# Layer 0's Gram matrices from float16 halves, a planner that knows of eight loads in flight, and a first batch turned row by row

## The chip, the cores and the metric

The kernel runs on one core of one Trainium2 chip. The metric is the device time in microseconds of one execution; the median of three runs is compared. PE is TensorE, DVE VectorE, ACT ScalarE, POOL GpSimd, SP SyncE. POOL issues the DMAs that convert a type, and SP most others.

## The reference, cut to what matters

Four graph layers work on `x` (16 batches of 1024 nodes with 128 features) and `adj` (16 x 1024 x 1024, zeros and ones). The change lies in layer 0:

```python
h = jnp.maximum(_layernorm(x, axis=-1), 0.0)
adjT = jnp.transpose(adj.astype(jnp.float32), (0, 2, 1))
w = _masked_row_softmax(adjT)                         # equal shares over a node's neighbours
region = jnp.matmul(w, h)
region = jnp.matmul(region, kernel_1) + bias_1        # 128 -> 256
region = _batch_norm(region, gamma_1, beta_1)         # mean and variance over all 16 x 1024 nodes
people = jnp.matmul(jnp.transpose(w, (0, 2, 1)), region)
people = jnp.matmul(people, kernel_2) + bias_2        # 256 -> 128
people = _batch_norm(people, gamma_2, beta_2)
x = x + people
```

Layers 1 to 3 are attention layers on the same `adj`.

## The kernel before

Since `adj` holds only zeros and ones, the softmax is a division by a node's number of neighbours. The kernel never forms `region @ kernel_1`. Both batch norms are worked out from sums: a 128x128 matrix of sums of squares and products (a Gram matrix) and column sums of the aggregated features, one pair for each norm. From these `norms` makes one folded 128x128 matrix, and only then can layers 1 to 3 start.

`first_layer` calls `batch(b)` sixteen times. A batch works as follows, with its steps by name and line:

- `load` (L372, POOL) brings eight blocks `a` of 128 rows of `adj`, 512 KB of int32 each, into 128 KB of 8-bit floats. There are 18 places for `a`. `load_x` (L366) brings the batch of x.
- `stats`, `aggregate` (L382, L386, DVE), `power` (L389, L390, POOL), `centre` (L394, DVE): layer norm. `upper` (L398, POOL) applies the ReLU and rounds to float16, `lower` (L401, DVE) keeps what the rounding left. The two float16 halves and a column of ones form `hv`, 257 wide.
- `turn` (L418, PE) transposes the blocks, 32 times 128x128. In each of four banks all eight blocks must be there. `square` (L426, ACT) writes the transposed matrix `at` and sums its rows, 8 times 1024 columns.
- `share` (L434 to L437, DVE) makes the reciprocals `rc`.
- `product` (L459, PE): eight blocks of eight matrix products with `hv`. Behind each block: `low` (L463, ACT), `join` (L467, DVE), giving `r`; then `high` (L471, POOL) and `rest` (L474, DVE) split `r` into the float16 halves `rv`.
- `spread` (PE, through `gram_product`, L352): eight float32 products of `r` with itself and a column of ones, added up in the bank `gram[0]` over all batches.
- `product2` (L499, PE): eight blocks of eight products of `at` with `rv`, 259 wide; `low2` (L503, ACT), `join2` (L506, DVE) give `g`; `spread2` adds up `gram[1]` (L352); `turn2` and `save` (L533 PE, L536 ACT) turn `g` back, and SP stores it.

Six banks `ps` hold the results of PE; the other two are the Gram matrices.

The order is not written by hand. `Plan` collects the steps, each with an engine, a duration in microseconds as the planner assumes it, and what it reads and writes. `attempt` lists the steps per engine: of those that could start within `L0_WITHIN` of the earliest, it takes the one with the smallest rank, which is the batch's due time (`L0_DUES`) less the length of the chain behind it. It also places the buffers. Instructions are then emitted in this order, and each engine runs its own in order. `norms` puts its steps in the same plan. `plain_layers` (layers 1 to 3) makes a plan of its own.

Before the plan, POOL writes the identity, the columns of ones and the constants (L242 to L344), and the loads follow.

Of the kernel before, what the change touches and what calls it, by code (L numbers as in the profile page):

```python
# [9 lines left out]
F16 = mybir.dt.float16  # L10
# [21 lines left out]

UP = 2.0**12
LEVEL = 1638.0
XG_TILES = 6
WEIGHTS_AT = 40.0
WHOLE = 4
L0_DUES, L0_WITHIN = [
    3.2, 51.2, 72.4, 90.5, 112.6, 124.5, 191.4, 204.9, 159.2, 265.6, 223.0, 273.4, 306.2, 325.8, 419.8, 408.3,
    419.5, 419.5,  # L40
], 0.1
# [173 lines left out]
def gnn_stack(ctx: ExitStack, tc: tile.TileContext, x, adj, k1, b1, g1, be1, k2, b2, g2, be2,  # L215
# [11 lines left out]
    ident = const.tile([P, P], F32, name="ident")  # L227
    make_identity(nc, ident)
    ident_h = const.tile([P, P], F16, name="ident_h")
    nc.vector.tensor_copy(ident_h, ident)  # L230
    ones = const.tile([P, P], F32, name="ones")
# [9 lines left out]
    rows9 = const.tile([P, P], BF16, name="rows9")  # L241
    nc.gpsimd.memset(rows9, 0.0)  # L242
    qall = const.tile([P, B, NB], F32, name="qall")
    q9_all = const.tile([P, B * NB * 9 + P - 9], BF16, name="q9_all")
    q9 = q9_all[:, : B * NB * 9].rearrange("p (b k c) -> p b k c", b=B, c=9)
    nc.gpsimd.memset(q9_all, 1.0)

# [60 lines left out]
def first_layer(tc, rooms, x, adj, adj_t, gt_rows, qall, ident, ident_h, mhalf, held):  # L308
# [7 lines left out]
    def places(kind, count, shape, dtype):  # L316
# [11 lines left out]
        "g": places("g", 2, [P, NB, D + 2], F32),  # L328
        "t": places("t", 2, [P, NB, D + 2], F32),
        "st": places("sta", 3, [P, NB, 6], F32),  # L330
        "mv": places("mva", 3, [P, NB, 2], F32),
# [5 lines left out]
    for t in kinds["hv"]:  # L337
        nc.gpsimd.memset(t[:, :, 2 * D : 2 * D + 1], 1.0)
    for t in kinds["rv"]:
        nc.gpsimd.memset(t[:, :, W2 - 1 : W2], 1.0)  # L340
    for t in kinds["r"]:
        nc.gpsimd.memset(t[:, :, D : D + 1], 1.0)
    for t in kinds["g"]:
        nc.gpsimd.memset(t[:, :, D + 1 : D + 2], 1.0)  # L344
    level = pool.tile([P, 1], F32, name="level")
    nc.vector.memset(level, -LEVEL)
    plan = Plan(kinds)
    plan.gram, plan.okay = gram, okay
    fresh = [True, True]

    def gram_product(k, lhs, rhs):
        nc.tensor.matmul(gram[k][:, : rhs.shape[1]], lhs, rhs, start=fresh[k], stop=True, skip_group_check=True)  # L352
        fresh[k] = False

    def batch(b):
# [9 lines left out]
        def load_x():  # L365
            queue.dma_start(xb.ap.rearrange("p (w t) d -> p w t d", t=2), x[b].rearrange(PAIRED, p=P, t=2))  # L366

        if b == 0:
            step(engine, us_, load_x, (), [xb, ("xo", b)], P * N * 4)
        for j in range(NB):  # L370
            def load(j=j):
                nc.gpsimd.dma_start(rows[j].ap, adj[b].rearrange(PAIRS_OF_ROWS, p=P, t=2)[j // 2, j % 2])  # L372

            step("pool", 0.6, load, (), [rows[j]], P * N * 4)
            if b and j == 1:
                step(engine, us_, load_x, [("xo", b - 1)], [xb, ("xo", b)], P * N * 4)

# [19 lines left out]
        def upper():  # L397
            nc.gpsimd.tensor_scalar_max(hv.ap[:, :, 0:D], y.ap, 0.0)  # L398

        def lower():  # L400
            nc.vector.scalar_tensor_tensor(hv.ap[:, :, D : 2 * D], y.ap, 0.0, hv.ap[:, :, 0:D],  # L401
                                           ALU.max, ALU.subtract)
# [4 lines left out]
        step("dve", 2.3, centre, [xb, mv, rs], [y])  # L407
        step("pool", 2.9, upper, [y], [(hv, 0)])
        step("dve", 1.2, lower, [y, (hv, 0)], [(hv, 1)])

        at, sums, rc = room("at"), room("col"), room("col")
        for w in range(NB // 2):
            ps = room("ps")

            def turn(w=w, ps=ps):
                t = ps.ap.bitcast(F16)
                for j in range(NB):
                    nc.tensor.transpose(t[:, j * P : (j + 1) * P],  # L418
                                        rows[j].ap.bitcast(F16)[:, w * P : (w + 1) * P], ident_h)

            step("pe", 0.47, turn, rows, [ps])
            for t in range(2):
                i = 2 * w + t

                def square(i=i, t=t, ps=ps):
                    nc.scalar.activation(at.ap[:, i, :], ps.ap.bitcast(F8)[:, t::2], AF.Square,  # L426
                                         saturate=False, accum_out=sums.ap[:, i : i + 1])

                step("act", 1.22, square, [ps], [(at, i), (sums, i)])

# [22 lines left out]
        for i in range(NB):  # L453
# [24 lines left out]
            def spread(i=i):  # L478
                gram_product(0, r.ap[:, i, :D], r.ap[:, i, :])

            step("pe", 0.95, product, [*rows, (hv, 0), (hv, 1)], [ps])
            step("act", 0.36, low, [ps, rc], [(t1, i)])
            step("dve", 0.29, join, [ps, rc, (t1, i)], [(r, i)])
            step("pool", 0.6, high, [(r, i), rc], [(rv, i, 0)])
            step("dve", 0.33, rest, [(r, i), rc, (rv, i, 0)], [(rv, i, 1)])
            step("pe", 0.23, spread, [(r, i)], [("gram", 0, b, i)])

# [6 lines left out]
        for j in range(NB):  # L494
            ps = room("ps")

            def product2(j=j, ps=ps):
                for i in range(NB):
                    nc.tensor.matmul(ps.ap[:, :W2], at.ap[:, i, j * P : (j + 1) * P],  # L499
                                     rv.ap[:, i, :], start=(i == 0), stop=(i == NB - 1))  # L500

            def low2(j=j, ps=ps):
                nc.scalar.copy(t2.ap[:, j, :], ps.ap[:, D + 1 : W2])  # L503

            def join2(j=j, ps=ps):
                nc.vector.tensor_tensor(g.ap[:, j, : D + 1], ps.ap[:, : D + 1], t2.ap[:, j, : D + 1],  # L506
                                        ALU.add)

            def spread2(j=j):
                gram_product(1, g.ap[:, j, :D], g.ap[:, j, :])  # L510

            step("pe", 0.95, product2,
                 [*((at, i) for i in range(NB)), *((rv, i, k) for i in range(NB) for k in (0, 1)), (rv, "c")],
                 [ps])
            step("act", 0.21, low2, [ps], [(t2, j)])
            step("dve", 0.25, join2, [ps, (t2, j)], [(g, j)])
            step("pe", 0.23, spread2, [(g, j)], [("gram", 1, b, j)])

        def open_rows():
            nc.vector.tensor_single_scalar(okay[:, b, 1, :], t2.ap[:, :, D + 1], 0.5, op=ALU.is_ge)  # L520

# [6 lines left out]
        for js in groups_of(NB, 4):  # L528
            ps = room("ps")

            def turn2(js=js, ps=ps):
                for k, j in enumerate(js):
                    nc.tensor.transpose(ps.ap[:, k * P : (k + 1) * P], g.ap[:, j, :D], ident)  # L533

            def save(js=js, ps=ps):
                nc.scalar.copy(gtr.ap[:, js[0] * P : (js[-1] + 1) * P], ps.ap)  # L536

            step("pe", 0.46, turn2, [(g, j) for j in js], [ps])
            step("act", 0.56, save, [ps], [(gtr, js[0])])
# [14 lines left out]
def norms(nc, plan, w, qall, q9, rows9, ident, ones, mhalf, gat1, gat3, edge, shift, kcs, flag, count):  # L554
# [100 lines left out]
    s1, v1, mean1, raw1, var1, sq1 = (tile_of(n, CB) for n in ("s1", "v1", "mean1", "raw1", "var1", "sq1"))  # L655
    dve(lambda: V.tensor_scalar_mul(cov, gram[0][:, : P + 1], UP**-2 / count), all1, [cov], 0.3)
    t3, m1 = plan.room("ps"), plan.room("ps")
# [10 lines left out]
    m2 = plan.room("ps")  # L668
    pe(means, [cov], [m1], 0.6)
    dve(lambda: V.tensor_tensor(gk, t3.ap[:, : CB * P], w["k1"], ALU.mult), [t3], [gk], 0.4)  # L670
# [23 lines left out]
    u9 = tile_of("u9", P)  # L694
    dve(lambda: V.tensor_scalar(u9[:9], u[:9], masks[:9, 3:4], 1.0 / UP, ALU.mult, ALU.mult), [u, "masks"], ["u9"], 0.2)
    dve(lambda: V.tensor_copy(uc, tc_.ap[:, 0:1]), [tc_], [uc])
# [5 lines left out]
    def q_sums():  # L702
        V.tensor_tensor(q2, qf, qf, ALU.mult)
        V.tensor_reduce(qs[:, 0:1], qf, AX.X, ALU.add)
        V.tensor_reduce(qs[:, 1:2], q2, AX.X, ALU.add)
        V.tensor_scalar_mul(qs[:, 0:1], qs[:, 0:1], 1.0 / UP / count)
        V.tensor_scalar_mul(qs[:, 1:2], qs[:, 1:2], UP**-2 / count)

# [21 lines left out]
    cov2, gk2, gq, gsum = tile_of("cov2", P), tile_of("gk2", P), tile_of("gq"), tile_of("gsum")  # L730
    dve(lambda: V.tensor_scalar_mul(cov2, gram[1][:, :P], UP**-2 / count), all2, [cov2], 0.25)
    dve(lambda: V.tensor_scalar_mul(gq, gram[1][:, P : P + 1], 2.0 * UP**-2 / count), all2, [gq])
    dve(lambda: V.tensor_scalar_mul(gsum, gram[1][:, P + 1 : P + 2], 1.0 / UP / count), all2, [gsum])
    t5, m3, m4 = plan.room("ps"), plan.room("ps"), plan.room("ps")
# [22 lines left out]
    pe(lambda: T.matmul(t7.ap[:, :P], ones, diag[1], start=True, stop=True), [diag[1]], [t7])  # L757
    dve(lambda: V.scalar_tensor_tensor(kcs, kc, 1.0 / UP, t6.ap[:, :P], ALU.mult, ALU.mult), [t6, kc], [kcs], 0.25)
    whole, rest2 = tile_of("whole", P), tile_of("rest2", P)
# [917 lines left out]
```

## Time and profile before

| what | value |
|---|---|
| median of three runs | 1424.29 us (1423.61 to 1425.9) |
| the profiled execution, its own time | 1423.44 us |
| span of its trace | 1421.6 us |
| granted TensorE clock, mean | 0.998 of full speed |
| PE, weight loads, DVE, ACT, POOL busy, share of the span | 97, 89, 77, 56, 25% |
| first transposition, first `product` | 7.44 us, 23.71 us |
| last Gram product of layer 0 | starts 362.27 us, takes 1.96 us |
| `product`, 64 matrix products of a batch | 7.18 us |
| `product2`, 64 | 7.24 us |
| one Gram matrix, one batch, 8 float32 products | 1.79 us |

The timeline lists groups of equal instructions with their start, their length from the first start to the last end, and in brackets the idle time in front of them with what ended it. The chain of waits follows the last instruction back to the first, and gives the starts and lengths of its pieces. A float32 matrix product shows as two instructions. A line that ends in "ld" for PE is a weight load, which overlaps the product before it.

### The profile page before, as it was taken

To read this page: it belongs to the slowest core of one execution; us is meant where nothing else is said; L and a number is where in the kernel's file an instruction comes from. 1 tells how busy PE (TensorE), PEld (TensorE's weight loads), DVE (VectorE), ACT (ScalarE), POOL (GpSimd) and SP (SyncE) were. 2 spreads that over 40 slices of the span, in tenths; PEclk is the share of its full clock that TensorE was granted. 3 is DMA by queue.
4 is the path that set the end of the run, shared out by engine and by line. 5 is a ranking of instruction groups with operands and counts; after the bars stand their busy time and mean duration, and the time that the engine had idled before them with its cause. 6 is when DMAs were issued, how large, how long until landed. Compare 5 with 4: busy or idle time off the path is not lost.

```text
span 1421.6 us, 30420 instructions
## 1 busy us (share of the span) xinstructions
PE 1373.0 (97%) x11710; PEld 1262.9 (89%) x11710; DVE 1100.7 (77%) x3148; ACT 794.2 (56%) x2123; POOL 358.9 (25%) x469
## 2 busy tenths in 40 slices
PE   4999999999999999999999999999999999999997
PEld 3889899899898898998899898998989998998897
DVE  4877666454688889887889788887888798977786
ACT  3766766666545645636374645546374655346643
POOL 7877676562210110201011101101011111020000
PEclk9999999999999999999999999999999999999999
DMA  9999887870300002121111112021221110000011
GB/s 157 146 186 170 116 167 149 112 99 7 119 2 16 31 31 75 46 90 60 46 60 46 64 41 75 31 80 47 84 60 60 60 46 31 31 1 16 16 44 65
DMA packets 56379, 99.05 MB, mean 70 GB/s; under 512 B 6328, under 2 KB 45600, under 8 KB 52896
## 3 DMA queue, kind: packets, MB, share of 16 engines
q1 hardware_dynamic: 37504, 79.17, 15.8%
q0 software_dynamic: 18720, 17.83, 14.5%
q8 instruction: 94, 1.54, 0.4%
q14 instruction: 61, 0.50, 0.1%
HBM read 118.37 MB, written 28.95 MB: 104 GB/s over the span
## 4 chain that ended last, share of the span: by engine, by line
PE 82%; DVE 8%; ACT 4%; POOL 2%; DMA 2%; issue 1%; DVEq 0%; ACTq 0%; POOLq 0%
PE psc L957 43%; PE psc L1100 7%; PE psa L499 7%; PE psa L459 7%; PE gram L352 4%; PE psc L1004 3%; PE psc L1132 3%; PE psc L933 2%; PE psa L418 2%; PE psc L882 1%; DVE xg L1068 1%; DMA a<-in_adj_dram 1%; DVE eu L1118 1%; ACT y L929 1%; POOL hv L398 1%
## 5 line engine op out<-in xcount | busy, mean ns | idle before, releaser
L957 PE MATMUL psc<-v,xg 128*128 128x129 f32 x4096 | 482.6, 275 | 1.3 <-DVE xg L1068 1.2
L957 PEld LDWEIGHTS psc<-v,xg 128*128 128x128 f32 x4096 | 471.7, 192 | 13.1 <-issue 7.3
L957 PEld LDWEIGHTS psc<-h,xg 128*128 128x128 f32 x2048 | 239.1, 192 | 16.9 <-DVE xg L1136 8.9
L957 PE MATMUL psc<-h,xg 128*128 128x129 f32 x2048 | 247.9, 276 | 3.8 <-DVE xg L1136 3.3
L915 POOL TENSOR_SCALAR col<-mv 128x8 f32<-128x8 f32 x48 | 20.9, 434 | 868.1 <-DVE mv L910 800.8
L1068 DVE SCALAR_TENSOR_TENSOR xg<-ub,tri,at 128x1024 f32<-128x1024 f32 x176 | 217.5, 1276 | 4.3 <-DMA at<-adj_t 2.9
L1108 ACT ACTIVATE eu<-psc,edge_shift 128x512 f32<-128x512 f32 x192 | 113.6, 592 | 173.5 <-PE psc L1100 173.0
L426 ACT ACTIVATE at<-psa 128x1024 fp8e4<-128x1024 fp8e4 x128 | 131.2, 1033 | 45.1 <-PE psa L418 43.3
L1100 PE MATMUL psc<-gt,gt 128*128 128x512 f32 (+3 forms) x384 | 150.9, 492 | 5.3 <-DVE xg L1136 4.0
L1118 DVE SCALAR_TENSOR_TENSOR eu<-e,edge_shift,eu 128x1024 f32<-128x1024 f32 (+7 forms) x128 | 104.0, 812 | 38.0 <-ACT e L1104 36.8
L459 PE MATMUL psa<-hv,a 128*128 128x257 f16 x1024 | 120.7, 277 | 3.3 <-DVE hv L401 3.3
L499 PE MATMUL psa<-rv,at 128*128 128x259 f16 x1024 | 120.0, 275 | 2.7 <-DVE g L506 2.2
L459 PEld LDWEIGHTS <-a 128*128 128x128 fp8e4 x1024 | 101.4, 99 | 19.1 <-issue 3.5
L499 PEld LDWEIGHTS <-at 128*128 128x128 fp8e4 x1024 | 99.6, 98 | 19.1 <-issue 3.6
L929 ACT ACTIVATE y<-xg,col 128x128 f32<-128x128 f32 x256 | 79.1, 400 | 65.1 <-DVE col L912 65.1
L1104 ACT ACTIVATE e<-psc,edge_shift 128x512 f32<-128x512 f32 x192 | 113.6, 592 | 0.0
L1068 DVE SCALAR_TENSOR_TENSOR xg<-ub,tri,atc 128x1024 f32<-128x1024 f32 x80 | 99.2, 1275 | 6.0 <-DMA ub<-u_rows 3.8
L1156 ACT ACTIVATE y<-psc,col 128x128 f32<-128x128 f32 x256 | 69.2, 419 | 56.5 <-DVE col L1150 56.3
L471 POOL TENSOR_SCALAR rv<-r,cola 128x128 f16<-128x128 f32 x128 | 82.0, 650 | 61.2 <-DVE r L467 61.0
L981 ACT ACTIVATE y<-psc,col 128x128 f32<-128x128 f32 x256 | 71.9, 394 | 45.3 <-DVE col L975 39.2
L916 POOL TENSOR_TENSOR col<-col,mhalf 128x8 f32<-128x8 f32 x48 | 94.1, 1961 | 4.0
L1060 ACT ACTIVATE v<-psc,col 128x128 f32<-128x128 f32 x256 | 72.4, 394 | 26.6 <-DVE col L1020 22.8
(209 smaller groups left out, 1941.9 us busy)
## 6 DMA issues: line engine op xcount, KB each, us to landing
a<-in_adj_dram POOLq DMA_DIRECT2D x128, 128.0 KB, 7.2
ub<-u_rows SPq DMA_DIRECT2D x29, 512.0 KB, 4.0
xb<-in_x_dram SPq DMA_DIRECT2D x27, 512.0 KB, 6.8
adj_t<-at SPq DMA_DIRECT2D x13, 1024.0 KB, 4.9
at<-adj_t SPq DMA_DIRECT2D x8, 1024.0 KB
out_dram<-y SPq DMA_DIRECT2D x15, 512.0 KB, 3.9
gt_rows<-xg SPq DMA_DIRECT2D x13, 512.0 KB, 5.6
xg<-gt_rows SPq DMA_DIRECT2D x13, 512.0 KB, 3.9
```

The costliest lines, as they stand in the source:

```text
L426: nc.scalar.activation(at.ap[:, i, :], ps.ap.bitcast(F8)[:, t::2], AF.Square, saturate=False, accum_out=sums.ap[:, i : i + 1])
L459: nc.tensor.matmul(ps.ap[:, : 2 * D + 1], block[:, i % 2 :: 2], hv.ap[:, j, :], start=(j == 0), stop=(j == NB - 1))
L471: nc.gpsimd.tensor_scalar_mul(rv.ap[:, i, 0:D], r.ap[:, i, :D], rc.ap[:, i : i + 1])
L499: nc.tensor.matmul(ps.ap[:, :W2], at.ap[:, i, j * P : (j + 1) * P], rv.ap[:, i, :], start=(i == 0), stop=(i == NB - 1))
L916: nc.gpsimd.tensor_tensor(rs.ap, va.ap, mhalf, ALU.pow)
L929: nc.scalar.activation(y.ap[:, n, :], xs(n), AF.Relu, bias=nm.ap[:, n : n + 1])
L957: nc.tensor.matmul(acc[g].ap[:, k * V1 : (k + 1) * V1], weights[m].ap[:, n * P : (n + 1) * P], values.ap[:, m, :], start=(m == 0 and k == ...
L1068: nc.vector.scalar_tensor_tensor(q[m].ap, ub.ap, ex.ap[:, m, 1:2], at.ap[:, m, :], ALU.max, ALU.mult)
L1100: nc.tensor.matmul(ps.ap[:, : len(c)], ha.ap[:, m * P : (m + 1) * P], ht.ap[:, m * P + c[0] : m * P + c[-1] + 1], start=True, stop=True)
L1104: nc.scalar.activation(e.ap[:, c[0] : c[-1] + 1], ps.ap[:, : len(c)], AF.Exp, bias=shift[:, 0:1], scale=1.0 - SLOPE)
L1108: nc.scalar.activation(eu.ap[:, ROW[m] + c[0] : ROW[m] + c[-1] + 1], ps.ap[:, : len(c)], AF.Exp, bias=shift[:, 1:2], scale=SLOPE)
L1118: nc.vector.scalar_tensor_tensor(t, e.ap[:, :wide], shift[:, 2:3], t, ALU.max, ALU.mult)
```

## The change

- Gram matrices: for batches 0 to 14 the float32 products go. `halves` splits all of `r` (later `g`) into two float16 halves `hl`: a copy on ACT, a subtraction on DVE, and for `g` two small operations for the column `q`. `gram_halves` makes two float16 products for each of the eight blocks: the first half with both halves and the columns of ones (259 wide), and the second half with itself and these columns (131 wide). All four kinds of products are thus kept. The last batch keeps float32 products (`gram_whole`), as one of 128 columns and one of the one or two others.
- `norms` adds the parts together (`sums`): the parts from batches 0 to 14 are prepared before the last batch's products are in.
- `g` is scaled down by 2^10 in `low2` and `join2` (which becomes a `scalar_tensor_tensor`), and the factors behind it follow (`UPG`).
- The planner: a load depends on the load eight places before it (`IN_FLIGHT`), the assumed durations of several steps and all due times are new.
- The first batch: each block is turned into all four banks as it arrives, and the ReLU is on ACT (`first_upper`) instead of POOL.
- POOL's constants go to DVE, and the identity is made behind the first loads.

```diff
+DOWN = 2.0**-10
+UPG = UP * DOWN
+IN_FLIGHT = 8
 L0_DUES, L0_WITHIN = [
-    3.2, 51.2, 72.4, 90.5, 112.6, 124.5, 191.4, 204.9, 159.2, 265.6, 223.0, 273.4, 306.2, 325.8, 419.8, 408.3,
-    419.5, 419.5,
+    0.3, 13.9, 23.7, 30.7, 41.0, 50.1, 58.8, 68.1, 75.2, 86.2, 96.1, 104.3, 114.0, 122.4, 148.4, 153.3, 151.6,
+    151.6,
 ], 0.1
...
-    make_identity(nc, ident)
-    nc.vector.tensor_copy(ident_h, ident)
-    nc.gpsimd.memset(rows9, 0.0)
+    nc.vector.memset(rows9, 0.0)
-    nc.gpsimd.memset(q9_all, 1.0)
+    nc.vector.memset(q9_all, 1.0)
...
+        "hl": places("hl", 2, [P, NB, 2 * D + 3], F16),
...
-    def gram_product(k, lhs, rhs):
-        nc.tensor.matmul(gram[k][:, : rhs.shape[1]], lhs, rhs, start=fresh[k], stop=True, skip_group_check=True)
+    def gram_add(k, at, lhs, rhs):
+        nc.tensor.matmul(gram[k][:, at : at + rhs.shape[1]], lhs, rhs, start=fresh[k], stop=True, skip_group_check=True)
         fresh[k] = False
+    def gram_whole(k, t, n):
+        gram_add(k, 0, t[:, n, :D], t[:, n, :D])
+        gram_add(k, 2 * D + 2 - k, t[:, n, :D], t[:, n, D:])
+    def gram_halves(k, t, n):
+        c = slice(0, 2 * D + 3)
+        gram_add(k, 0, t[:, n, :D], t[:, n, c])
+        gram_add(k, 2 * D + 3, t[:, n, D : 2 * D], t[:, n, D : 2 * D + 3])
...
+        def begun():
+            sent[0] += 1
+            return ([("sent", sent[0] - IN_FLIGHT)] if sent[0] >= IN_FLIGHT else []), ("sent", sent[0])
...
-            step("pool", 0.6, load, (), [rows[j]], P * N * 4)
+            limit, mine = begun()
+            step("pool", 0.55, load, limit, [rows[j], mine], P * N * 4)
+            if b == 0 and j == 3:
+                step("pool", 0.6, lambda: make_identity(nc, ident), (), ["ident"])
+                step("dve", 0.3, lambda: nc.vector.tensor_copy(ident_h, ident), ["ident"], ["ident_h"])
...
+        def first_upper():
+            nc.scalar.activation(hv.ap[:, :, 0:D], y.ap, AF.Relu)
...
-            step("pe", 0.47, turn, rows, [ps])
+        if b == 0:
+            for j in range(NB):
+                step("pe", 0.25, lambda j=j: turn(range(NB // 2), [j]), [rows[j], "ident_h"], turned)
...
-                step("act", 1.22, square, [ps], [(at, i), (sums, i)])
+                step("act", 1.0, square, [ps], [(at, i), (sums, i)])
...
-            step("pe", 0.23, spread, [(r, i)], [("gram", 0, b, i)])
+            if b == B - 1:
+                step("pe", 0.34, spread, [(r, i)], [("gram", 0, b, i)])
+        def halves(k, t, width):
+            hl = room("hl")
+            def first():
+                nc.scalar.copy(hl.ap[:, :, :D], t.ap[:, :, :D])
+            def second():
+                nc.vector.tensor_tensor(hl.ap[:, :, D : 2 * D], t.ap[:, :, :D], hl.ap[:, :, :D], ALU.subtract)
+                if k:
+                    nc.vector.tensor_copy(hl.ap[:, :, 2 * D + 1], t.ap[:, :, D])
+                    nc.vector.tensor_tensor(hl.ap[:, :, 2 * D], t.ap[:, :, D], hl.ap[:, :, 2 * D + 1], ALU.subtract)
+            step("act", 1.0, first, [(t, i) for i in range(NB)], [(hl, 0)])
+            step("dve", 1.6 if k else 1.2, second, [*((t, i) for i in range(NB)), (hl, 0)], [(hl, 1)])
+            for i in range(NB):
+                step("pe", 0.17, lambda i=i: gram_halves(k, hl.ap, i), [(hl, 0), (hl, 1)], [("gram", k, b, i)])
+        if b < B - 1:
+            halves(0, r, D)
...
-                nc.scalar.copy(t2.ap[:, j, :], ps.ap[:, D + 1 : W2])
+                nc.scalar.mul(t2.ap[:, j, :], ps.ap[:, D + 1 : W2], DOWN)
...
-                nc.vector.tensor_tensor(g.ap[:, j, : D + 1], ps.ap[:, : D + 1], t2.ap[:, j, : D + 1],
-                                        ALU.add)
+                nc.vector.scalar_tensor_tensor(g.ap[:, j, : D + 1], ps.ap[:, : D + 1], DOWN, t2.ap[:, j, : D + 1],
+                                               ALU.mult, ALU.add)
...
-    dve(lambda: V.tensor_scalar_mul(cov, gram[0][:, : P + 1], UP**-2 / count), all1, [cov], 0.3)
+    def sums(k, cov, scale, all_):
+        low = tile_of(f"low{k}", P + 3)
+        early = [a for a in all_ if a[2] < B - 1]
+        act(lambda: S.mul(low, gram[k][:, 2 * P + 3 : 3 * P + 6], scale), early, [low], 0.4)
+        dve(lambda: V.scalar_tensor_tensor(low[:, :P], gram[k][:, P : 2 * P], 2.0 * scale, low[:, :P], ALU.mult, ALU.add),
+            [low, *early], [low], 0.35)
+        dve(lambda: V.scalar_tensor_tensor(cov[:, :P], gram[k][:, :P], scale, low[:, :P], ALU.mult, ALU.add),
+            [low, *all_], [cov], 0.35)
+        return low
```

## The prediction

> **What bounds it now.** I read the page first, then the window table of layer 0 in steps of 20 us, the chain of waits, the timeline of the first 60 us, and single groups. Times: the profiled execution took 1423.44 us, its span is 1421.6, and the median of the runs is 1424.29, 0.85 above the profiled one; I sum against the profiled run and add 0.85 at the end.
>
> The page's busy line and its chain, by engine, come first.
>
> ```profile
> PE 1373.0 (97%) x11710; PEld 1262.9 (89%) x11710; DVE 1100.7 (77%) x3148; ACT 794.2 (56%) x2123; POOL 358.9 (25%) x469
> ...
> PE 82%; DVE 8%; ACT 4%; POOL 2%; DMA 2%; issue 1%; DVEq 0%; ACTq 0%; POOLq 0%
> ```
>
> TensorE sets the time. The window table shows where that holds in layer 0.
>
> ```profile
> 0.00:20.00 20.00, 4.45 (x31) 3.17 (x32) 4.64 (x29) 3.40 (x6) 14.07 (x36) 1.00 0.95 115
> 20.00:40.00 20.00, 16.70 (x142) 13.87 (x141) 14.61 (x54) 13.31 (x30) 16.02 (x18) 1.00 0.96 182
> 40.00:60.00 20.00, 17.91 (x163) 15.71 (x162) 17.82 (x89) 11.08 (x28) 16.03 (x22) 1.00 1.05 188
> ...
> 160.00:180.00 20.00, 20.00 (x196) 18.08 (x194) 12.56 (x55) 14.18 (x33) 13.64 (x20) 1.00 1.00 166
> 180.00:200.00 20.00, 20.00 (x196) 18.20 (x194) 12.79 (x55) 14.14 (x34) 13.95 (x20) 1.00 0.92 163
> ```
>
> The columns are PE, weight loads, DVE, ACT, POOL, granted clock, DMA share. From about 51 us to 351 PE is full and the clock whole: a us taken off PE there is a us gained, as long as nothing else becomes late. Before 51 us PE has holes, so the head is ruled by latency. The chain gives PE's prices per batch.
>
> ```profile
> 59.11 1.79 PE psa L418 x32
> ...
> 188.14 7.24 PE psa L499 x64
> 195.38 1.79 PE gram L352 x16
> 198.04 7.18 PE psa L459 x64
> ```
>
> A batch is 1.79 (turning) + 7.18 + 7.24 + 2 x 1.79 (both Gram matrices) + 1.04 (L533, eight in 1.04 in the timeline) = 20.8 us.
>
> **Gram products of batches 0 to 14.** Eight float32 products take 1.79, 0.224 each, in two instructions each. The new pair is a float16 product 259 wide and one 131 wide. L499 is exactly 259 wide with a float16 moving side: 7.24/64 = 0.113. L418 is the nearest to 131: 1.79/32 = 0.056 for 128, so 0.057. Eight pairs: 8 x 0.170 = 1.36, a saving of 0.43 per matrix and batch, 30 times: **-12.8 us**, all in the full stretch. Both rows include their weight loads. I keep 0.40 to 0.45 as bounds, 12.0 to 13.5.
>
> **What pays for it.** Each matrix adds an ACT copy of 128x1024 (L1084, 1.06) and a DVE subtraction (L401, same size, 1.23), g's also two 128x8 operations (L435, 0.20). `join2` becomes the form of `join`: 0.35 for 0.29, 0.5 in eight. Per batch DVE gets 2.5 + 0.4 + 0.5 = 3.4 on 13.5 (51.52 busy in 160 to 240 us, per 20.8), ACT 2.1 on 14.8, in a new period of 20.0: 84% each. PE covers it, so the work costs nothing unless it is late.
>
> Late for whom? In the changed order PE does, behind the last block of `product`, g's pairs of the batch before (1.36), its turning back (1.04) and 24 turns (1.34): 3.7 us, then r's pairs. These need the last `low` (0.46), `join` (0.35), the copy (1.06) and the subtraction (1.23), and three hops of 0.1 (a `join` ended at 179.16, its `high` began at 179.26): 3.4; in some batches DVE's queue has `full` and the statistics (1.64) in front of the subtraction, which started behind `join` makes 4.3. So 0 to 0.6 a batch is exposed, and `product2` waits in line behind r's pairs. Float32 products needed only `join`. I take 0.17 a batch, **+2.6 us**, bounds 0 and 9.
>
> There is a second price. DVE's operation with two inputs in SBUF can hold up POOL: these two POOL steps took 1.95 where one alone takes 0.61, beside `lower`.
>
> ```profile
> 48.94 1.95 POOL L471 TENSOR_SCALAR rv<-r,cola 128x128 f16<-128x128 f32 x2
> ...
> 49.20 1.22 DVE L401 SCALAR_TENSOR_TENSOR hv<-ya,hv 128x1024 f16<-128x1024 f32 x1
> ```
>
> So 0.7 us were lost once. In the changed order r's subtraction lies between the `rest` steps, where POOL's `high` run: 15 x 0.7 = 10 us of POOL at most. `product2` has some 5.6 us of other PE work in front of it and its last `high` is due about 5 behind `product`, so most is hidden; the 9 above takes it in.
>
> The Trainium skill, "SBUF — State Buffer", section "Who interferes with whom", is sterner: a VectorE instruction with two SBUF inputs takes the shared read port for its whole length, and a GpSimd instruction that reads SBUF blocks fully. By it each of the 30 subtractions could hold POOL for its 1.23 us, 37 us of POOL, and and with a third of that on the path the sum, by this estimate, would end near 1426. The row above shows a partial block, and its 0.7 is what I use.
>
> **Last batch.** Batch 15 keeps float32 products, now 128 wide, and adds for each a product of one or two columns with its own weight load.
>
> ```profile
> 354.83 0.58 PE L666 MATMUL psa<-ones,gk 128*128 128x1 f32 x4 [0.34 <-DVE raw L672]
> ```
>
> Four such instructions in 0.58; a product has two: 0.2 to 0.29. Sixteen: 3.2 to 4.6, I take 3.4. Both matrices lie on the path: r's at 350.87, where PE is full, g's at 362.27, after the last `join2`. In `norms` the sums of batches 0 to 14 are merged early; on the path one multiply-add (0.35) replaces a scaling (0.29), and gq and gsum the same: 0.2. Together **+3.6**, 3 to 5.5.
>
> **Head.** Rows before:
>
> ```profile
> 7.68 0.53 POOL L372 DMA_DIRECT2D a<-in_adj_dram  x1 [0.42 <-DMA a<-in_adj_dram]
> 14.88 1.68 POOL L390 TENSOR_TENSOR cola<-cola,mhalf 128x8 f32<-128x8 f32 x1
> 17.56 2.85 PE L418 MATMUL psa<-ident_h,a 128*128 128x128 f16 x25 [0.94 <-DMA a<-in_adj_dram]
> 19.56 2.84 POOL L398 TENSOR_SCALAR hv<-ya 128x1024 f16<-128x1024 f32 x1
> 30.39 2.21 ACT L463 ACTIVATE t<-psa,level,cola 128x129 f32<-128x129 f32 x6 [4.36 <-DVE cola L435]
> 32.83 5.61 POOL L471 TENSOR_SCALAR rv<-r,cola 128x128 f16<-128x128 f32 x8
> ```
>
> The ninth load already waits for the first to land, so eight in flight adds no wait; only places change. The first load is issued at 2.74 behind the memsets; with these on DVE it goes at about 0.75. Rows then land some 2 us earlier, the last at 15.6 instead of 17.56 (the first batch of x shares the wires, so perhaps 16.5). `power` stands behind ten loads, not twelve: about 8.6 to 10.5 instead of 14.60. `centre` 2.1, ReLU on ACT 1.1 instead of POOL's 2.84, `lower` 1.2: the halves of h are ready at 15, so `product` starts near 16, not 23.71. All four banks have been turned by 16; eight squares of 1.0 end at 24; the reciprocals come at 25, not 30. `join` then runs to 29, but POOL's eight `high` now have six loads of 0.55 between them, and DVE puts `centre` and the subtraction (3.4) in front of the last five `rest`: `product2` starts near 35, against 38.87. By then PE has done 12.2 us of work and lost 23; before, it had lost 26.9 when it became full at 51.44 (24.5 us of work done). That, and little in the next batch, where r's `join` stands behind `centre` and g's subtraction, gives **-3.4 us**; bounds -7.7 (all of the earlier start) and +1. The memsets that go to DVE (2.0 us on POOL) fit before x lands there at 4.81. `ident` is made behind nine loads, near 6.5 us, so the turning of the first row waits about 1 us more than its landing; rows come 1.25 us apart and four turns take 0.3, so it has caught up by the third row. If that cover were gone, it would cost that 1 us.
>
> Everything after layer 0 stands in the same order on every engine. Sum: -12.8 + 2.6 + 3.6 - 3.4 = **-10.0**: 1413.4 for the profiled run, 1414.3 for the median, said as 1414.0.
>
> **Rivals.**
> - *The halves are late (slower).* PE waits at r's pairs in each batch, since copy and subtraction queue behind the statistics and `centre`. Break-even is 10.0 + 2.6 = 12.6 us, 0.84 a batch. If the copy and subtraction were wholly bare, 15 x 2.3 = 34 us: 1414 + 32 = 1446. For: the 3.7 against 4.3 above, two engines at 84%. Against: one or two blocks of the next `product` (0.9 each) stand before `product2` in many batches and take up a part. Chance 0.09: 0.06 slower, 0.03 about even.
> - *The head gives all.* Start 7.7 earlier kept and no wait exposed: -12.8 + 3.6 - 7.7 = -16.9, 1407. For: what delayed the first `product` before, 17.56 to 23.71, were POOL's `power` and `hv`, and both are off its late queue. Against: the six loads between the `high`. 0.20.
> - *DMA becomes the bound.* 0.92 busy from 160 to 240 us is 19.2 us of a period of 20.8; a period of 20.0 leaves 4%. If loads in bursts of eight can't fill it, the pair's saving is lost: 1425. Against: the share falls to 0.11 from 320 us on, 40 us before PE's last Gram product. 0.04.
> - *It doesn't do what it says* for the eight in flight: true as worked out, worth nothing by itself.
>
> **How the numbers follow.** The main case has 0.67, its own range 1409 to 1420. Of the rest, the head's rival draws the lower end to 1405, the late halves the upper to 1422, leaving some 0.15 outside. A measurement here tells 0.2% (2.8 us) from no change: faster is below 1421.4, slower above 1427.1. Faster 0.67 + 0.20 less 0.02 of the main case's tail = 0.85; same 0.02 + 0.03 + 0.04 = 0.09; slower 0.06.
>
> **What would show it.** Right: the line of the Gram products takes 1.36 instead of 1.79 a batch and matrix; PE full from about 48 us to the norms, with holes of 0.2 us a batch; `product` from 16, `product2` from 35; the last batch's Gram products near 3.5 a matrix; the last of them ending near 354 instead of 364.2. Wrong: idle of PE in front of r's pairs or `product2` with DVE's subtraction named, pairs at over 0.2 each, or loads as releasers behind 60 us.

## The result and the profile after

The changed kernel takes 1429.51 us (median; 1426.9 to 1432.96), the kernel before beside it 1423.55. The ratio is 1.0044, with a 95% interval of 1.0032 to 1.0056: slower by 0.4%, where 0.7% faster was forecast. The profiled execution took 1429.69 us, its span is 1427.8, 6.2 longer than before. Layers 1 to 3 stand in the same order as before, and the last Gram product of layer 0 ends 6.1 us later, at 370.3 instead of 364.2. So the loss lies in layer 0.

The page's busy line after, and the shares of the chain by engine:

```profile
PE 1368.8 (96%) x11742; PEld 1250.4 (88%) x11742; DVE 1151.0 (81%) x3227; ACT 825.0 (58%) x2156; POOL 368.2 (26%) x458
...
PE 76%; DVE 10%; ACT 7%; POOL 3%; DMA 2%; issue 2%; SPq 0%; DVEq 0%; ACTq 0%; POOLq 0%
```

TensorE works 4 us less and yet the kernel is longer. Its share of the chain fell from 82 to 76%, and DVE, ACT and POOL took over what it lost. The window table shows where; its columns are those of the table of before:

```profile
0.00:20.00 20.00, 7.30 (x46) 4.98 (x47) 7.47 (x42) 5.26 (x8) 12.68 (x26) 1.00 0.98 123
20.00:40.00 20.00, 15.01 (x118) 11.97 (x117) 13.68 (x50) 14.27 (x31) 15.52 (x22) 0.83 1.10 186
...
100.00:120.00 20.00, 16.80 (x170) 14.39 (x168) 16.43 (x67) 13.93 (x32) 15.87 (x22) 1.00 0.93 157
...
160.00:180.00 20.00, 19.41 (x196) 17.05 (x194) 17.41 (x64) 17.36 (x38) 14.23 (x20) 1.00 0.80 147
```

PE is not full where it was: from 60 to 260 us it was busy for 199.4 of 200 us before and 186.1 after. In the same stretch DVE went from 135.7 to 165.8, ACT from 137.7 to 150.7, POOL from 146.6 to 153.0. The second row also shows a granted clock of 0.83, where before had 1.00.

Who keeps PE waiting is in the list of waits of layer 0 (microseconds in total, times, the longest one):

```profile
PE psa L559 <- DVE g L566: 5.9, 7, 1.7
PE psa L559 <- ACT at L464: 4.4, 5, 0.9
PE gram L357 <- DVE hl L535: 3.9, 2, 3.7
```

Before, the first of these was 2.2 in total, 1.8 of it in the head, and the second absent. The subtraction that I had watched (L535) is named mainly once, in the head. Elsewhere it is `product2` (L559) that waits, and for a bank: six banks circulate, and one comes free only when `join2` (L566) has read it or, where it holds turned blocks, when the squares (L464) have. The timeline of one such place:

```profile
109.46 1.07 ACT L464 ACTIVATE at<-psa 128x1024 fp8e4<-128x1024 fp8e4 x1
...
111.45 0.35 ACT L563 ACTIVATE t<-psa 128x130 f32<-128x130 f32 x1
111.66 0.67 DVE L472 TENSOR_SCALAR cola<-cola 128x8 f32<-128x8 f32 x1 [0.58 <-ACT at L464]
111.68 1.06 PE L559 MATMUL psa<-rv,at 128*128 128x259 f16 x8 [0.93 <-ACT at L464]
113.12 2.62 DVE L421 TENSOR_SCALAR ya<-xb,mva,cola 128x128 f32<-128x128 f32 x8
113.25 1.06 PE L559 MATMUL psa<-rv,at 128*128 128x259 f16 x8 [0.51 <-DVE g L566]
115.66 0.48 DVE L566 SCALAR_TENSOR_TENSOR g<-psa,t 128x129 f32<-128x129 f32 x2
115.99 4.69 PE L559 MATMUL psa<-rv,at 128*128 128x259 f16 x40 [1.67 <-DVE g L566]
```

Read from the top: eight squares fill ACT's queue from 103.46 to 111.4, and `low2` (L563) stands behind them. On DVE `share` (L472) waits for the last square; behind it come one `join2` and then `centre` (L421) for 2.62 us, and the next `join2`, at 115.66, stand behind that. So two blocks of `product2` each run alone, with 0.93, 0.51 and 1.67 us of idle PE around them.

### The profile page after: what moved, and what is told of

The parts are those of the page before. It is cut to its first block, busy times and chain, and to the rows that moved or that the text cites. A ratio compares the mean times of both kernels' runs of the same rounds, so it can differ in the third digit from the quotient of the medians.

```text
span 1427.8 us, 30566 instructions
## 1 busy us (share of the span) xinstructions
PE 1368.8 (96%) x11742; PEld 1250.4 (88%) x11742; DVE 1151.0 (81%) x3227; ACT 825.0 (58%) x2156; POOL 368.2 (26%) x458
## 4 chain that ended last, share of the span: by engine, by line
PE 76%; DVE 10%; ACT 7%; POOL 3%; DMA 2%; issue 2%; SPq 0%; DVEq 0%; ACTq 0%; POOLq 0%
PE psc L1045 43%; PE psc L1188 7%; PE psa L559 6%; PE psa L497 5%; PE psc L1092 3%; PE psc L1220 3%; PE gram L357 2%; PE psc L1021 2%; ACT at L464 2%; PE psc L970 1%; DVE xg L1156 1%; ACT y L1017 1%; DVE ya L421 1%; DVE eu L1206 1%; POOL rv L509 1%
## 5 line engine op out<-in xcount | busy, mean ns | idle before, releaser
L559 PE MATMUL psa<-rv,at 128*128 128x259 f16 x1024 | 123.2, 276 | 12.9 <-DVE g L566 5.9
L464 ACT ACTIVATE at<-psa 128x1024 fp8e4<-128x1024 fp8e4 x128 | 129.9, 1038 | 3.1 <-PE psa L451 3.1
L559 PEld LDWEIGHTS <-at 128*128 128x128 fp8e4 x1024 | 100.3, 98 | 32.9 <-issue 14.6
L509 POOL TENSOR_SCALAR rv<-r,cola 128x128 f16<-128x128 f32 x128 | 86.0, 692 | 31.7 <-DVE r L505 31.1
```

The lines of the kernel that those rows point to most:

```text
L509: nc.gpsimd.tensor_scalar_mul(rv.ap[:, i, 0:D], r.ap[:, i, :D], rc.ap[:, i : i + 1])
```

## The experiments

All ratios are to the kernel before on the same chip. "PE 60–260" is PE's busy time in that stretch (before: 199.4 us; changed: 186.1).

| run | time, us | ratio, 95% interval | PE 60–260 |
|---|---|---|---|
| halves_only | 1452.28 | 1.0195, 1.0179 to 1.0211 | 184.5 |
| all_but_halves | 1444.46 | 1.0141, 1.0125 to 1.0156 | 186.5 |
| old_planner | 1437.21 | 1.0093, 1.0077 to 1.0108 | 186.4 |
| measured | 1430.22 | 1.0047, 1.0033 to 1.0061 | 184.1 |
| searched | 1422.32 | 0.9992, 0.9983 to 1.0001 | 191.5 |
| float32_searched | 1429.38 | 1.0045, 1.0031 to 1.0059 | 195.6 |
| after_rounded | 1444.20 | 1.0145, 1.0130 to 1.0161 | 182.8 |
| before_rounded | 1428.60 | 1.0034, 1.0021 to 1.0048 | 197.5 |
| small_second | 1423.13 | 0.9998, 0.9989 to 1.0007 | 189.1 |
| small_both | 1423.87 | 1.0005, 0.9996 to 1.0015 | 188.7 |
| one_input | 1426.17 | 1.0022, 1.0013 to 1.0031 | 188.5 |
| warm | 1427.39 | 1.0034, 1.0021 to 1.0048 | 186.9 |
| one_product | 1417.67 | 0.9959, 0.9946 to 0.9973 | 190.9 |
| whole_once | 1418.78 | 0.9965, 0.9951 to 0.9978 | 191.5 |
| whole_once_warm | 1416.75 | 0.9955, 0.9942 to 0.9969 | 191.2 |

### Which part costs: the halves, the plan or the head

**halves_only** is the kernel before with the halves alone (its planner, due times and first batch kept).

> Kernel before, with nothing but the float16 halves added (their steps, the scale of g, the merged sums); its own head, planner, assumed durations and due times. Theory A (the new order is what costs; the halves take 9 us off PE as forecast): 0.6% faster than before, about 1415 us, PE idle behind 60 us as small as before. Theory B (the added ACT and DVE work makes PE wait whatever the order): 0.4% slower or more, 1428 to 1440 us, with PE waiting for DVE's g, for ACT's squares and for the halves from 60 us on.

**all_but_halves** is the changed kernel with float32 Gram products again:

```diff
-        gram_add(k, 0, t[:, n, :D], t[:, n, :D])
-        gram_add(k, 2 * D + 2 - k, t[:, n, :D], t[:, n, D:])
+        gram_add(k, 0, t[:, n, :D], t[:, n, :])
...
-        if b < B - 1:
-            halves(0, r, D)
```

> The changed kernel with float32 Gram products in all batches, as before: new head, planner, durations and due times stay. Theory A: slower than before by some 10 us (the new order's stalls stay, the 9 us of the halves are lost), 1433 to 1440 us. Theory B: the head's 2 to 4 us are kept and nothing else is late: 1418 to 1422 us.

**old_planner** is the changed kernel with the assumed durations and due times of before, and no dependency between loads.

> The changed kernel with the durations, due times and load dependencies that the planner had before; halves and head are kept. Theory A: the fastest of these, 1410 to 1414 us. Theory B: within 5 us of the changed kernel, 1425 to 1434 us.

No part is the culprit. Added to the kernel before, the halves cost 28 us; taking them out of the changed kernel costs 15 (1444.46 against 1429.51). The same steps, then, have two signs, and what differs is the order around them. The waits of halves_only show the one that I had forecast as a rival, in front of r's and g's pairs, and beside it the one for a bank:

```profile
PE gram L359 <- DVE hl L526: 9.6, 13, 2.6
PE psa L550 <- DVE g L557: 9.0, 14, 3.1
```

old_planner loses 7.7 us more than the changed kernel, so its new plan serves the new steps better than the old one. Yet even with the new plan PE is idle for 13.9 of the 200 us.

### How much the order alone decides

**measured** gives the planner the durations of the trace where they had been short:

```diff
-            step("pool", 0.6, high, [(r, i), rc], [(rv, i, 0)])
-            step("dve", 0.33, rest, [(r, i), rc, (rv, i, 0)], [(rv, i, 1)])
+            step("pool", 0.7, high, [(r, i), rc], [(rv, i, 0)])
+            step("dve", 0.44, rest, [(r, i), rc, (rv, i, 0)], [(rv, i, 1)])
```

and the same for `power`, `share`, `low`, `join`, the halves, `low2`, `join2` and `turn2`.

> The changed kernel, its planner given durations as the changed trace shows them: high 0.70 for 0.60, rest 0.44 for 0.33, power 2.3 for 2.0, share 1.0 for 0.7, low 0.42 for 0.36, low2 0.27 for 0.21, join 0.33 for 0.29, join2 0.28 for 0.25, the halves 1.05, 1.25 and 1.75. Due times unchanged. Theory A in the form that the order was made for a POOL and a DVE faster than they are: PE's stalls behind 60 us fall by half, 1419 to 1424 us. Theory B: no better than the changed kernel, 1427 to 1433 us.

**searched** keeps these durations and has eighteen other due times, found by a search. **float32_searched** does the same for all_but_halves, with `L0_WITHIN` at 0.3.

> The changed kernel with the same instructions, planned with the durations of the run 'measured' and with other due times (5.7, 14.3, 24.4, 29.1, 38.4, 48.6, 56.2, 62.4, 85.4, 90.7, 103.1, 112.8, 124.5, 135.9, 146.1, 152.3, 151.2, 152.0), found by a search: only the order differs. Theory A (the order costs, not the added work): 1415 to 1421 us, faster than before, and PE idle behind 60 us falls from 14 to below 6 us. Theory B (the added ACT and DVE work and what it does to POOL cost it in any order): 1427 us or more.

> The same for the float32 Gram products: all but the halves, planned with the durations of 'measured', and with due times of their own from a search of the same length (0.8, 8.2, 19.4, 25.8, 36.3, 53.9, 62.1, 72.1, 81.3, 111.8, 120.2, 141.2, 149.6, 170.2, 178.2, 189.8, 177.6, 190.7; window 0.3). Theory A: 9 to 12 us behind 'searched', near the kernel before, 1423 to 1432 us. Theory B: ahead of 'searched'.

Right durations alone bring nothing. Other due times bring 7.2 us against the changed kernel, with not one instruction changed. The waits of searched show which of the two went:

```profile
PE psa L559 <- ACT at L464: 5.2, 6, 1.1
PE psa L559 <- DVE g L566: 1.4, 3, 0.7
```

The bank behind `join2` fell from 5.9 to 1.4 us; the one behind the squares stayed. With an order searched for each, the halves are worth 7.1 us (1422.32 against 1429.38), some three quarters of the 9.2 (-12.8 + 3.6) of the forecast for the pairs and the last batch. That figure hangs on the search: for the float32 products it found no order as good as that of the kernel before, which makes the same products with the old first batch in 5.8 us less (1423.6). Against the kernel before, searched gains 1.3 us, and its interval reaches no change. PE is still idle for 8.5 of 200 us in searched, and for 4.4 in float32_searched.

**after_rounded** and **before_rounded** change due times only, and only by rounding: the changed kernel's to multiples of 2 us, those of before to multiples of 10.

```diff
-    0.3, 13.9, 23.7, 30.7, 41.0, 50.1, 58.8, 68.1, 75.2, 86.2, 96.1, 104.3, 114.0, 122.4, 148.4, 153.3, 151.6,
-    151.6,
+    0, 14, 24, 30, 40, 50, 58, 68, 76, 86, 96, 104, 114, 122, 148, 154, 152, 152,
```

> The changed kernel with every due time of layer 0 rounded to a multiple of 2 us, nothing else: the same instructions in another order. Theory A (the order decides, and the changed kernel's due times fit its own steps only): slower than the changed kernel by 6 to 14 us, 1435 to 1443 us. If the order hardly mattered: within 2 us of it.

> The kernel before with its eighteen due times rounded to multiples of 10 us, and nothing else changed; its order alone differs. Theory (the order before is one of the few that leave TensorE no wait, and so every edit of the steps that moves it gives up some of that): slower by 3 to 15 us, 1427 to 1438, with TensorE's waits for a bank back in the trace. Rival (the kernel before is tolerant of its order, and what was lost in the changed kernel is its own steps' doing): within 2 us of 1423.6.

The rival is out: the kernel before loses 5.4 us by rounding its due times, and PE's wait for a bank behind the squares, which its own trace has not, is back:

```profile
PE psa L458 <- ACT at L425: 4.1, 5, 0.9
```

The full PE of before thus belonged to its fitted order, and not to the steps alone. The changed kernel is more sensitive still: a much smaller rounding costs it 14.7 us (part of that is work at a lower clock, 0.97 on average from 60 to 260 us). That goes with its fuller queues in the window table (DVE 83% instead of 68%, ACT 75% instead of 69%, POOL 76% instead of 73% from 60 to 260 us); that the fuller queues are the reason was not tried by itself.

### What the split itself costs

**small_second** cuts the subtraction to one column for each block, **small_both** the copy as well, **one_input** puts a reduction of the same length with one input in its place. The order is that of the changed kernel.

```diff
-                nc.vector.tensor_tensor(hl.ap[:, :, D : 2 * D], t.ap[:, :, :D], hl.ap[:, :, :D], ALU.subtract)
+                nc.vector.tensor_reduce(hl.ap[:, :, D : D + 1], t.ap[:, :, :D], AX.X, ALU.max)
```

> The changed kernel in the same order on every engine, but the subtraction that makes the second half covers 8 elements a row instead of 1024 (the second halves are left out; both hl tiles are filled with ones at the start). DVE is freed of 30 x 1.0 us, POOL of what these hold up. Theory A: the joins still stand behind centre and the squares, so little comes back: 1424 to 1428 us. Theory B: most of PE's idle goes: 1414 to 1419 us.

> As small_second, and ACT's copy that makes the first half also covers 8 elements a row (both halves are left out, the products on PE stay). ACT is freed of 30 x 0.85 us besides. Theory A: 1422 to 1427 us. Theory B: 1409 to 1416 us, at least 3 us below small_second, as ACT's squares and low2 come earlier.

> The changed kernel in the same order, but the subtraction is replaced by a reduction over 1024 elements: about the same 1.2 us on DVE, with one SBUF input instead of two (the second halves are left out). Theory P (the second SBUF input holds up POOL's steps, and this is what the subtraction costs): as small_second, 1422 to 1425 us, and high and rest back to a mean below 0.66 and 0.40 us. Theory D (it is DVE's time that costs): as the changed kernel, 1428 to 1431 us.

Without the subtraction this order gains 6.4 us, and without the copy nothing more (the intervals of small_second and small_both overlap). With one input 3.3 of the 6.4 come back, but these are not the second input's alone. The Gram pairs that start at 61.73 us in the changed kernel start at 60.05 in one_input and 57.22 in small_second, and the last Gram product, at 366.63, starts at 362.74 and 359.61. So 4.5 of the 7.0 us between the traces of the changed kernel and small_second lie in the head, where the first subtraction is on the path and the granted clock differs too (0.83, 0.91 in one_input and 1.00 in small_second from 20 to 40 us). Behind 60 us the subtraction costs 2.5 us, and one_input returns 2.2 of them. Even these are an upper bound for the second input: the reduction doesn't read ACT's copy, so DVE's wait for it (11.9 us from 60 to 340 us in the changed kernel, 13.0 in small_second) is gone in one_input. The two were not separated.

The groups of POOL's `high` from 60 to 340 us, of the changed kernel, of small_second and of one_input, show what a second input does (mean ns behind the bar's sum):

```profile
L509 POOL TENSOR_SCALAR rv<-r,cola 128x128 f16<-128x128 f32 x107 | 72.1, 695 | 27.4 <-DVE r L505 26.9
```

```profile
L509 POOL TENSOR_SCALAR rv<-r,cola 128x128 f16<-128x128 f32 x106 | 65.4, 641 | 24.4 <-DVE r L505 23.8
```

```profile
L509 POOL TENSOR_SCALAR rv<-r,cola 128x128 f16<-128x128 f32 x107 | 66.3, 644 | 26.8 <-DVE r L505 26.2
```

A reduction of the same 1.22 us leaves `high` about as fast as no subtraction does. The mean hides how the loss comes about: the median `high` takes 0.617 us in the changed kernel and 0.614 in one_input. Seven of the 107 are held by a subtraction that runs beside them: they take 0.91 to 1.75 us, each ending 0.39 to 0.48 us behind it; together they lose some 5.6 us, which is nearly all that lies between the sums 72.1 and 66.3. One of them is the first of the two here; it takes 0.91 us and ends at 83.04, 0.47 behind the subtraction beside it:

```profile
81.34 1.23 DVE L535 TENSOR_TENSOR hl<-r,hl 128x1024 f16<-128x1024 f32 x1 [0.52 <-ACT hl L532]
82.13 1.50 POOL L509 TENSOR_SCALAR rv<-r,cola 128x128 f16<-128x128 f32 x2
```

In one_input a `high` that begins at 270.16 us, inside the reduction of 270.01, takes 0.60.

### The clock behind the idle gap of the head

**warm** does three of the four turnings of batch 1 three times over, in PE's gap near 30 us:

```diff
-                for j in js:
+                for j in (list(js) * 3 if b == 1 and w < 3 else js):
```

> The changed kernel in the same order; in batch 1 three of the four turnings are done three times over (the same values into the same banks), 2.7 us of PE work in the 3.7 us in which PE waits for the first halves near 30 us. Theory C (that gap lowers the granted clock to 0.83 between 20 and 40 us and makes the work behind it slower): clock 1.00 there, 1.5 to 2.5 us faster, 1427 to 1428 us. Otherwise no change or up to 0.5 us slower.

The timeline of the changed kernel and that of warm, at the first pairs and the first `product2`:

```profile
33.66 2.77 PE L357 MATMUL gram<-hl 128*128 128x259 f16 x16 [3.69 <-DVE hl L535]
...
37.08 3.17 PE L559 MATMUL psa<-rv,at 128*128 128x259 f16 x18
```

```profile
33.45 1.53 PE L357 MATMUL gram<-hl 128*128 128x259 f16 x16 [1.00 <-DVE hl L535]
...
35.26 7.66 PE L559 MATMUL psa<-rv,at 128*128 128x259 f16 x64
```

Behind 3.69 us of idling the same sixteen products take 2.77 instead of 1.53 us; with the gap filled the clock of that window is 1.00 and `product2` begins 1.8 us earlier; the pairs at 61.73 us start at 59.18. The time falls by 2.1 us. The two intervals overlap, as do those of whole_once and whole_once_warm below, where it is 2.0 us; what speaks for the clock is that both pairs agree with the rows, and that each execution of whole_once_warm (1415.61 to 1417.2 us) is below each of whole_once (1417.24 to 1419.38). The medians carry other falls of the clock too: its mean lies between 0.993 and 0.998 in single executions of the changed kernel.

### One product for each block of the last batch

**one_product** is searched with the halves laid the other way round in their tile, so that `gram_whole` is one product again. In it r's column of ones in `hl` lies where g's `q` is written, so the column sums of r are others. **whole_once** gives r a place of its own for them, and **whole_once_warm** adds the repeated turnings.

```diff
-        gram_add(k, 0, t[:, n, :D], t[:, n, :D])
-        gram_add(k, 2 * D + 2 - k, t[:, n, :D], t[:, n, D:])
+        gram_add(k, 0, t[:, n, :D], t[:, n, :])
...
-        "r": places("r", 2, [P, NB, D + 1], F32),
+        "r": places("r", 2, [P, NB, D + 2], F32),
```

> 'searched' with the columns of hl in another order (first half, the three columns, second half), so that the last batch's float32 product is one of 129 or 130 columns again instead of two. Same order of steps. The term of the last batch in the prediction (3.4 us) comes back: 3 to 3.5 us faster than 'searched', 1419 us, which beats the kernel before by 0.3%.

> The searched order (1422.3 us) with one change behind it: the float16 halves lie the other way round in their tile and the last batch's float32 Gram products go over r and its ones at once, so that each matrix of the last batch takes one product where two stood for each block. Theory of the last batch (its two products for each block cost 3.4 to 4.6 us on the path): 1418 us, 1417 to 1419.5, and below the kernel before by 0.3%. Rival (the last batch's products are hidden, because the chain behind them waits for VectorE): 1421.5 to 1423.

> whole_once with the turnings of batch 1 repeated three times in the gap near 30 us, which keeps TensorE's clock at 1.00 there. Theory (the clock costs 2 us in any order, since the products behind it are on the path): 1.5 to 2.5 us below whole_once, near 1416. Rival (the 2 us were the order's, shifted into a better place, and not the clock's): within 1 us of whole_once or above it.

The Gram products of the last batch in the timeline, in the changed kernel and in whole_once_warm:

```profile
351.67 3.63 PE L357 MATMUL gram<-r 128*128 128x128 f32 x32
...
366.63 3.71 PE L357 MATMUL gram<-g 128*128 128x128 f32 x32
```

```profile
344.68 2.01 PE L357 MATMUL gram<-r 128*128 128x130 f32 x16
...
356.80 1.96 PE L357 MATMUL gram<-g 128*128 128x130 f32 x16
```

They fall by 1.62 and 1.75 us, and the kernel by 3.5 (1422.32 to 1418.78): both matrices lie bare on the path. whole_once_warm, at 1416.75 us, beats the changed kernel by 12.8 us and the kernel before by 0.45%.

## Why the prediction was wrong

**The failed step is the stall term, "I take 0.17 a batch, +2.6 us, bounds 0 and 9".** (The sum itself gives 1414.3 for the median; it was said as 1414.0.) I count PE's lost time as elapsed time less the work done, at the full-speed rows. Up to 60 us it is 27.5 us after and 27.4 before. Behind 60 us, up to the last Gram product, it is 18.6 against 3.2: +15.4, 1.0 us a batch. The sum then reads -12.8 + 3.6 + 15.4 + 0.1 = +6.3, and the span grew by 6.2.

Three things went wrong in that step.

- It asked for one wait only: whether r's pairs would be late for copy and subtraction. They hardly were. The waits that came are those of `product2` for a bank. The sentence that "PE covers it, so the work costs nothing unless it is late" was applied to the new steps, and not to the old ones (`low2`, `join2`) that now stand behind squares, `share` and `centre` in the same queues.
- It took "From about 51 us to 351 PE is full" for slack that the kernel has. before_rounded shows that the same steps in a neighbouring order lose 5 us. A new order had to be expected to have stalls of its own, and the new due times say only that the planner's assumed durations fitted, not the chip's.
- The second price, 0.7 us of POOL for each of r's subtractions, came from a row read as a partial block. In that row the second `high` begins at 49.54 us and ends at 50.89, 0.47 behind the end of `lower` at 50.42: it was held for all that was left of `lower`. The rule of the Trainium skill ("SBUF — State Buffer", "Who interferes with whom"), that two inputs block POOL's reads and a reduction does not, agrees with that row and with the `high` beside the subtraction and the reduction. What made the 37 us of the estimate too much is that few subtractions hold a `high`: seven of 27 from 60 to 340 us, some 5.6 us of POOL. On the path behind 60 us one_input puts the second input at 2.2 us at most, so it is a small part of the 15.4.

**The head, -3.4, gave nothing.** Up to the first `product` it held: 17.16 instead of 23.71 (16 forecast). What I passed over is the stretch behind it, in the chain of waits of the changed kernel:

```profile
17.08 8.16 ACT at L464 x16
...
30.04 2.44 DVE ya L421 x8
33.66 2.77 PE gram L357 x16
```

The squares rule until 25, then `centre` stands in front of the first subtraction. PE idles for 3.69 us and comes back at a lower clock, which I had at nothing; warm puts that at about 2 us. `product2` starts at 37.08, where 35 was forecast.

**The Gram pairs held, -12.8.** Eight pairs show as 1.53 us in the timeline, which counts to the end of the last one; the work behind them starts earlier. For the pairs at 61.73 us the next product starts at 63.09, 1.36 later, which is the forecast. The saving is there, and was spent on waits.

**The last batch held, +3.6.** 3.63 and 3.71 us for 3.5 each; taking the second product away returned 3.5.

**The rivals.** The outcome has the sign of "the halves are late", and the break-even of 0.84 us a batch was passed at 1.0, but through another wait. Its place as I described it shows in halves_only alone. DMA is not the bound: its share stays at 0.77 to 0.93 from 100 to 180 us, and no load is named as a releaser of PE behind 60 us. "The head gives all" was the farthest off, since the head gave nothing. Of the listed signs for "wrong" the right one came, idle PE in front of `product2`, but with other steps named: `join2` and ACT's squares, not the subtraction. The work forecast for DVE held (84% of a period; 85% from 160 to 240 us, the stretch that it was worked out from), and ACT came to 79% there for 84; the conclusion from it did not hold.

Open is whether an order exists in which the changed steps leave PE without a wait: the best one found still loses 8.5 us of 200, so of the 15.4 us of lost PE time the runs show about half (7.2 us of the kernel's time) to be the order's alone.

## What to carry to other kernels

When a fitted order makes the bounding engine full, that fullness belongs to the order. An edit that adds steps to the neighbouring queues, or makes the planner choose anew, should be charged with the stalls of an unfitted order first (here 5 to 15 us, found by rounding the due times), and its saving compared only after both versions have an order searched for them; and where the search does not find an order as good as the old one for the old steps, as here, the old kernel stays the mark. Ask of each queue that gets new work which old step behind it frees a buffer, and not only when the new step's own result is due.

## What the runs showed of the hardware that I had not expected

- After 3.69 us of idling, sixteen Gram products took 2.77 us instead of 1.53, and the granted clock of that 20 us window was 0.83; filling the gap with repeated transpositions kept it at 1.00. The Trainium skill ("TensorE: Matmul & The Clock Gate", "What's actually happening") has the clock fall to half after an idle window of some 3.4 us; this place agrees: behind the gap `product2` starts with products 0.22 us apart, and behind 39.2 us they stand 0.11 apart. The column does not show the low clock at the start of a kernel: it reads 1.00 from 20 to 40 us in the kernel before, and yet the first 64 products take 9.90 us there, for 7.18 in a later batch; the first 23 stand 0.21 us apart, those behind 28.9 us 0.11:

```profile
23.71 9.90 PE L459 MATMUL psa<-hv,a 128*128 128x257 f16 x64 [3.30 <-DVE hv L401]
```

- A 128x128 `high` on POOL that ran into a subtraction with both inputs in SBUF was held to its end and took 0.91 to 1.75 us instead of 0.61; beside a reduction of the same length, with one input, the median stayed at 0.61.
